# A graph layer's edge scatter: block rows picked from three stacked bfloat16 parts, and the feeding that goes with it

## The chip, the cores and the metric

The kernel runs on one core of a Trainium2 chip. The metric is the device time of one execution in microseconds; a chip run gives it, and a hardware profile of one execution gives the trace.

## The reference

A message-passing layer with 12500 nodes of 64 features, 212500 edges sorted by `dst`, and a hidden width of 128 (float32 throughout):

```python
h = jnp.maximum(_layernorm(x, axis=-1), 0.0)
edge_in = jnp.concatenate([h[src], h[dst], edge_weight1], axis=1)
e = jax.nn.silu(edge_in @ eW1 + eb1)
e = jax.nn.silu(e @ eW2 + eb2)
agg = jax.ops.segment_sum(e, src, num_segments=12500)
out = jax.nn.silu(jnp.concatenate([h, agg], axis=1) @ nW1 + nb1) @ nW2 + nb2
return x + out
```

The edges come sorted by `dst` but the sum runs over `src`, so the kernel has to bring each edge's half-finished row from its place by `dst` to a place by `src`.

## The kernel before

`eW1` is cut in its `src` part, its `dst` part, its weight row and bias. Tables of h times the first two parts are built once per node (`ta` and `tb` in DRAM, and `tb0` for the first nodes; `product` makes them for groups of four tiles of nodes: `first_rows` for `tb0`, `by_edges` and `groups` for the rest).

**Sending.** The edges are taken in 208 blocks of 1024, two to a pair. Since `dst` is sorted, a block's edges need only few rows of `tb`: each quarter of a block (256 edges) has a window of 30 rows. `load_rows` (SP) loads the block's row numbers within the windows, spread over the partitions (`bc`), `windows` loads the window rows (`win`, four transfers a pair), `weights` loads the edge weights as a row of `pick`. `count` (DVE, and PE for `counts`) works out where each edge goes (`to`), and makes `pick`, at L410 for a pair at once: a one-hot matrix of 0 and 1 from `bc`, with the weight row and a row of ones beside it. `send` then works in four pieces per block. PE multiplies `pick` by `win` (`qp`, L477, float32, 64 rows of contraction in two halves): that picks each edge's row of `tb` and adds weight and bias. ACT copies it to the tile `qs` (L486, and a column of places, L487; 16 buffers), and POOL scatters `qs`, 128 edges at a time, to the rows `to` of the array `q` in DRAM (L490, an indirect DMA; 1661 in all).

**Steps.** 450 steps, in 18 levels of 25 batches of nodes, read `q` back by `src` (`qt`, SP), add the rows of `ta`, and run the two layers and the segment sum: `lr` (L598), `oneT` (L603), `pt` (L612, L618), silu (L622), `p` (L650), silu (L654), `seg` (L664), `aggT` (L675).

**What sets the order.** The program order on each engine is written by hand. `turn` lists a step's parts; its empty places (`None`) are where pieces of `send` are put in, so many that the rows which a later level needs are scattered in time. Before the steps begin, 16 blocks are sent, with table building fed in between pieces by counts such as

```python
            for i in range(2, 2 * PIECES):
                next(sending)
                for _ in range(3 if i % PIECES < 3 else 0):
                    next(feed, None)
```

A scatter holds its `qs` buffer and its `to` buffer (four) until it has landed. Each engine works through its own list in order, so an instruction that waits holds up all behind it on that engine.

Of the kernel before, what the change touches and what calls it, by code (L numbers as in the profile page):

```python
# [38 lines left out]
P = 128  # L39
L = 125  # L40
WL = 30
STEP = 15
SPAN = 7 * STEP + WL
# [21 lines left out]
FILL0, FILL_EACH, FILL_LATE = 18, 2, 8  # L65
AFTER = mybir.DependencyInfo(mybir.DependencyClass.Sync, mybir.DependencyReason.DATA)
# [8 lines left out]
def tile_gnn(ctx: ExitStack, tc: tile.TileContext, x, src, dst, ew, eW1, eb1, eW2, eb2, nW1, nb1, nW2, nb2, out):  # L75
# [155 lines left out]
    wins = [const.tile([P, 2, 2, H], F32, name=f"win{i}") for i in range(NW)]  # L231
    nc.vector.memset(wins[0], 0.0)

    def extra_rows(dma, wins):

        for win in wins:
# [69 lines left out]
    qsp = ctx.enter_context(tc.tile_pool(name="qs", bufs=16))  # L306
    top = ctx.enter_context(tc.tile_pool(name="to", bufs=4))
    with ExitStack() as work:
# [19 lines left out]
        def load_rows(s):  # L328

            if s < nblocks:  # L330
# [5 lines left out]
                if g == 0:  # L336
                    bc = ld.tile([P, 2, QR], BF16, name="bc")
                    lists[p] = [bc, None]
                    r = dests[p, 0, 0]
                    of = bass.AP(tensor=r.tensor, offset=r.offset, ap=[[2 * QR, NQR], [0, 32], [1, 2 * QR]])  # L340
                    nc.sync.dma_start(bc.rearrange("p g e -> p (g e)"), of)
                blk[s] = [lists[p][0][:, g]]

        def windows(p):

            table, front, end = (tb, FRONT, NB * P) if 2 * p >= EARLY else (tb0, 0, NE * P)
            if p == 0:
                table, end = tb0[: FRONT + G * P], G * P
            assert 2 * p < EARLY or len(done_b) == NB // G
            at = nc.sync.value_load(base_i[:, p : p + 1], min_val=front, max_val=FRONT + end - SPAN)  # L350
            for a in range(NQR):
# [3 lines left out]
                nc.sync.dma_start(wins[p % NW][a * 32 : a * 32 + WL, :, a % 2, :], of)  # L355

        def load(s):

            if s < nblocks:
                p, g = s // 2, s % 2  # L360
                if g == 0:
                    if p != 1:
                        windows(p)
                    lists[p][1] = ld.tile([P, 2, QR], F32, name="pick")
                blk[s] += [wins[p % NW][:, g], lists[p][1][:, g]]
            if s:
                load_rows(s + 1)

        def weights(s):

            if s < nblocks:
                p, g = s // 2, s % 2
                pick = lists[p][1][:, g]
                e0 = s * BLK
                m = 1 if e0 + 2 * BLK > E else 2
                if m == 2 or e0 + BLK <= E:
                    of = bass.AP(tensor=ew.tensor, offset=ew.offset + e0, ap=[[QR, NQR], [BLK, m], [1, QR]])
                    nc.sync.dma_start(lists[p][1][WL::32, g : g + m, :], of)
                else:
                    for a in range(NQR):  # L380
                        m = min(QR, E - e0 - a * QR)
                        if m > 0:
                            of = bass.AP(tensor=ew.tensor, offset=ew.offset + e0 + a * QR, ap=[[m, 1], [1, m]])
                            nc.sync.dma_start(pick[a * 32 + WL : a * 32 + WL + 1, :m], of)

        def count(s):

            if s < nblocks:
                bc, win, pick = blk[s]
                p, g = s // 2, s % 2  # L390
                whole = p > 0 and (2 * p + 2) * BLK <= E
# [15 lines left out]
                elif not whole:  # L407
                    nc.vector.tensor_scalar(pick, bc, same, plus, op0=OP.is_equal, op1=OP.add)
                elif g == 0:
                    nc.vector.tensor_scalar(lists[p][1], lists[p][0], same, plus, op0=OP.is_equal, op1=OP.add)  # L410
            yield
            if s < nblocks and p and (g == 0 or not whole):
                weights(s)
# [45 lines left out]
        def send(s):  # L459
# [6 lines left out]
            places = locE[:, g * TB : (g + 1) * TB, p].rearrange("p (i a t) -> p i t a", a=2, i=2)  # L466
            for t, i in itertools.product(range(2), range(2)):
                if i or t:
                    yield
                if i == 0:  # L470
# [9 lines left out]
                tiles = [j for j in (4 * i + t, 4 * i + 2 + t) if j < nt]  # L480
# [3 lines left out]
                qp = qps[i]  # L484
# [235 lines left out]
        def first_rows(g):  # L720

            hr = turned(x0, g)
            yield
            got = fp.tile([P, G, H], F32, name="got")
            product(1, hr, mm, "mm", got)
            yield
            nc.scalar.dma_start(tb0[FRONT + g * P : FRONT + (g + G) * P, :].rearrange("(p j) f -> p j f", j=G), got)
# [12 lines left out]
        def products(b0, g, xs):  # L740
# [7 lines left out]
            else:  # L748
                rows_a = fp.tile([P, G, H], F32, name="rows_a")
# [8 lines left out]
            nc.sync.dma_start(tb_buckets[:, b : b + G, :], got)  # L758
# [15 lines left out]
        def destinations():  # L774
# [9 lines left out]
            nc.vector.tensor_scalar(few, part[:NP], 0.5, -float((NE - G) * P), op0=OP.is_lt, op1=OP.mult)  # L784
# [11 lines left out]
            for g in range(2):  # L796
                nc.vector.tensor_tensor(
                    rowsD[:, :, g, :],
# [12 lines left out]
        def first_places():  # L811
# [8 lines left out]
            for at, rows in ((slice(0, 1), G * P), (slice(1, FIRST), NE * P)):  # L820
# [76 lines left out]

        def checks():
# [24 lines left out]
        done_a, done_b, ready, scaled = [], [], set(), set()  # L923
# [321 lines left out]
```

## Time and profile before

| | |
|---|---|
| median of 3 runs | 2332.47 us (2330.95 to 2333.67) |
| the profiled execution | 2332.11 us, span 2330.3 us |
| granted TensorE clock, mean | 0.958 |
| busy | PE 2091.2, PEld 1842.1, DVE 1864.6, ACT 1180.1, POOL 1649.9 us |
| DMA | 401.86 MB, 172 GB/s on the mean |

PE is a matmul's own time and PEld the loading of weights beside it; DVE, ACT and POOL are the vector, scalar and GpSimd engines, SP issues DMAs. A row `A <- B: total, times, longest` of the waits says that an engine's line A stood idle until B ended. "issue" is idle time with nothing to wait for in the trace. A row of the timeline begins with its start and its duration in microseconds.

### The profile page before, as it was taken

What the parts mean: (1) busy time and instruction counts of PE and PEld (TensorE: products, weight loads), DVE (VectorE), ACT (ScalarE), POOL (GpSimd) and SP (SyncE); (2) the same over time, 40 slices, a digit from 0 to 9 for tenths busy, and PEclk for the clock granted to TensorE, in tenths of its full rate; (3) what the DMA queues carried; (4) which work ended last, traced back from release to release, by engine and by line L of the source; (5) the groups of instructions that cost most, each with busy time, mean ns of one, the idle gap of its engine ahead of it and who ended that gap; (6) DMA issues with size and microseconds to landing.
All of it is one profiled execution on the core that took longest, in us unless ns stands there. A gap on an engine that the chain in (4) does not pass through costs nothing.

```text
span 2330.3 us, 49976 instructions
## 1 busy us (share of the span) xinstructions
PE 2091.2 (90%) x17399; PEld 1842.1 (79%) x17399; DVE 1864.6 (80%) x3292; ACT 1180.1 (51%) x3262; POOL 1649.9 (71%) x1711
## 2 busy tenths in 40 slices
PE   3685998889999999998899889999888999999998
PEld 2463677778988888887788778888778888889997
DVE  6975677778888889888888878888888888887664
ACT  3364554445555555554455555555555555555443
POOL 5677777777777777777777777777777777777210
PEclk9766899899999999999999999999999999999999
DMA  4476676555555565555555555555654444444563
GB/s 137 152 240 206 223 248 193 178 185 182 179 179 174 179 180 183 180 174 172 160 169 176 171 169 180 168 169 173 188 168 137 137 138 139 140 139 139 167 211 117
DMA packets 241432, 401.86 MB, mean 172 GB/s; under 512 B 47528, under 2 KB 140195, under 8 KB 240965
## 3 DMA queue, kind: packets, MB, share of 16 engines
q1 hardware_dynamic: 149411, 216.21, 31.6%
q0 software_dynamic: 53568, 123.20, 14.7%
q10 hardware_dynamic: 38192, 59.17, 8.7%
q8 instruction: 139, 2.28, 0.4%
q14 instruction: 122, 1.00, 0.1%
HBM read 191.09 MB, written 207.01 MB: 171 GB/s over the span
## 4 chain that ended last, share of the span: by engine, by line
PE 47%; DMA 20%; DVE 18%; issue 6%; POOL 5%; ACT 3%; SPq 1%; DVEq 0%; ACTq 0%; POOLq 0%
DMA q<-qs,to 14%; PE seg L664 10%; PE pt L618 10%; PE p L650 8%; DMA qt<-q 5%; PE pt L612 5%; PE qp L477 5%; POOL q L490 5%; PE lr L598 3%; DVE one L631 3%; DVE oneT L603 2%; DVE aggT L675 2%; DVE each L400 2%; DVE oh L395 1%; PE ab L215 1%
## 5 line engine op out<-in xcount | busy, mean ns | idle before, releaser
L490 POOL DMA_INDIRECT q<-qs,to x1661 | 1621.8, 976 | 546.2 <-issue 316.8
L622 ACT ACTIVATE e<-pt 128x512 f32<-128x512 f32 x450 | 268.7, 597 | 769.4 <-PE pt L618 680.6
L664 PE MATMUL seg<-one,e 128*128 128x125 f32 x3600 | 496.4, 281 | 34.2 <-DVE aggT L675 24.1
L664 PEld LDWEIGHTS seg<-one,e 128*128 128x128 f32 x3600 | 440.7, 193 | 106.8 <-issue 35.2
L650 PE MATMUL p<-w,e 128*128 128x128 f32 x3600 | 486.7, 278 | 0.0
L650 PEld LDWEIGHTS p<-w,e 128*128 128x128 f32 x3600 | 442.7, 193 | 12.1 <-issue 10.5
L486 ACT COPY qs<-qp 128x256 f32<-128x256 f32 x831 | 308.9, 372 | 221.0 <-PE qp L477 212.6
L675 DVE TENSOR_TENSOR aggT<-aggT,seg 128x500 f32<-128x500 f32 x425 | 284.3, 669 | 87.4 <-PE seg L664 85.7
L603 DVE TENSOR_SCALAR oneT<-lr,part 125x512 f32<-125x512 f32 x450 | 335.2, 745 | 22.9 <-PE lr L598 17.3
L477 PE MATMUL qp<-win,pick 64*128 64x256 f32 x1662 | 318.1, 453 | 14.2 <-ACT qs L486 5.8
L631 DVE TENSOR_TENSOR one<-counts,qt 128x500 f32<-128x500 f32 x450 | 300.9, 669 | 25.6 <-PE counts L434 14.3
L612 PE MATMUL pt<-ident,qt 128*128 128x128 f32 x1800 | 283.7, 281 | 1.5 <-ACT zn L267 1.3
L654 ACT ACTIVATE e<-p 128x512 f32<-128x512 f32 x450 | 269.1, 598 | 30.2 <-PE p L650 18.0
L644 ACT COPY p<-b2f 128x512 f32<-128x512 f32 x450 | 267.7, 595 | 0.0
L618 PE MATMUL pt<-oneT,al 125*128 125x128 f32 x1952 | 264.2, 279 | 0.0
L618 PEld LDWEIGHTS pt<-oneT,al 125*128 125x128 f32 x1952 | 243.6, 196 | 0.0
L449 DVE TENSOR_TENSOR mine<-oh,counts 128x800 f32<-128x800 bf16 x208 | 203.6, 979 | 41.1 <-PE counts L434 41.1
L598 PEld LDWEIGHTS <-qt 128*125 128x125 bf16 x1800 | 156.0, 140 | 84.7 <-DMA qt<-q 49.8
L598 PE MATMUL lr<-identb,qt 128*125 128x128 bf16 x1800 | 185.0, 226 | 39.1 <-DMA qt<-q 37.9
L612 PEld LDWEIGHTS pt<-ident,qt 128*128 128x128 f32 x1800 | 194.8, 144 | 29.3 <-issue 22.5
L451 DVE TENSOR_REDUCE rank<-mine 128x8 f32<-128x800 f32 x208 | 205.1, 986 | 7.2
L400 DVE TENSOR_REDUCE each<-oh 128x100 bf16<-128x800 bf16 x208 | 205.1, 986 | 7.1
(177 smaller groups left out, 1780.4 us busy)
## 6 DMA issues: line engine op xcount, KB each, us to landing
qt<-q SPq DMA_DIRECT2D x450, 288.0 KB
q<-zeros ACTq DMA_DIRECT2D x70, 720.0 KB
q<-qs,to POOLq DMA_INDIRECT x1661
bc<-dests SPq DMA_DIRECT2D x103, 128.0 KB
win<-tb SPq DMA_DIRECT2D x416, 30.0 KB
tb<-got SPq DMA_DIRECT2D x25, 256.0 KB
zd<-zn SPq DMA_DIRECT2D x25, 250.0 KB
zh<-zd SPq DMA_DIRECT2D x25, 250.0 KB
```

The lines of the kernel that those rows point to most:

```text
L477: nc.tensor.matmul(qps[i_][:, :m], pick[half, t * P : (t + 1) * P], win[half, :m], start=True, stop=True)
L486: nc.scalar.copy(qs[:, :m, :H], qp[:, :m, :])
L490: ins = nc.gpsimd.indirect_dma_start(out=q[:], out_offset=bass.IndirectOffsetOnAxis(ap=to[:k, j : j + 1], axis=0), in_=qs[:k, a, :], in_of ...
L598: nc.tensor.matmul(lr[:L, t, :], loc[:, at : at + 1].to_broadcast([P, L]), identb, start=True, stop=True)
L603: nc.vector.tensor_scalar(oneT, st[k].pop("lr")[:L], part1[:L, :], None, op0=OP.is_equal)
L612: nc.tensor.matmul(pt[:, t, :], qt[:, j, :H], ident, is_transpose=True, start=t == 0, stop=False, skip_group_check=True)
L618: nc.tensor.matmul(pt[:, cols, :], a[:L, b, :], oneT[:, cols, :], start=False, stop=True, skip_group_check=True)
L631: nc.vector.tensor_tensor(one.rearrange("p (b j) l -> p b j l", j=n), nodes_p[:, None, None, :].to_broadcast(wide), loc[:, tiles[0][1] : t ...
L650: nc.tensor.matmul(p2[:, t, :], e1[:, t, :], w2, start=False, stop=t == G - 1, skip_group_check=True)
L654: nc.scalar.activation(e2, p2, AF.Silu)
L664: nc.tensor.matmul(item[2][:, b, :], e2[:, t, :], one[:, t, :], start=j < G, stop=j >= G * (n - 1))
L675: nc.vector.tensor_tensor(v, v, seg, op=OP.add)
```

## The change

- `tb` and `tb0` hold, for each row, three bfloat16 numbers that add up to the float32 (`split`: ACT casts, DVE subtracts, ACT casts the rest, DVE subtracts). Block 0 and 1 keep the float32 way from a table of their own (`tbF`, `win0`, `pick0`).
- A pair's windows come in one transfer: 32 rows, each with its three parts, on 96 partitions, eight windows of 128 edges. Its row numbers come on 96 partitions for all 2048 edges (`picks`), and DVE turns them into 0 and 1 in place. Below them, 12 partitions hold three parts of the weights and ones, against three parts of the weight row and the bias (`weighs`, `extra`, made by `first_weights` and `other_weights`).
- A tile of 128 edges then takes one product of 108 rows by 128, in bfloat16.
- `qs` has 9 buffers where it had 16, `rows_a` 2; the lists of `src` and `dst` are cast in place, and `src`'s buffer is loaded again with the weights.
- The feeding counts are others, and `first_weights`, `first_rows` and the rest take turns.

```diff
+    same3 = const.tile([P, 1], F32, name="same3")
+    nc.vector.tensor_scalar(same3, part, -1.0, 1.0 / 3, op0=OP.add, op1=OP.mult)
+    nc.vector.tensor_scalar(same3, same3, float(3 * 2**22), None, op0=OP.add)
+    nc.vector.tensor_scalar(same3, same3, -float(3 * 2**22), None, op0=OP.add)
...
-    tb = dram.tile([P * NB, H], F32, name="tb")
-    dests = dram.tile([NP, NQR, 2, QR], BF16, name="dests")
-
-    tb0 = dram.tile([FRONT + P * NE, H], F32, name="tb0")
+    tb = dram.tile([P * NB, 3 * H], BF16, name="tb")
+    dests = dram.tile([NP, 2 * NQR, QR], BF16, name="dests")
+    weighs = dram.tile([4, NP * PAIR], BF16, name="weighs")
+    extra = dram.tile([12, H], BF16, name="extra")
...
+    def split(*pairs_):
+
+        with nc.allow_low_precision("three parts hold every bit"):
+            for parts, v in pairs_:
+                nc.scalar.copy(parts[0], v)
+            yield
+            for parts, v in pairs_:
+                nc.vector.tensor_tensor(v, v, parts[0], op=OP.subtract)
+            yield
+            for parts, v in pairs_:
+                nc.scalar.copy(parts[1], v)
+            yield
+            for parts, v in pairs_:
+                nc.vector.tensor_tensor(parts[2], v, parts[1], op=OP.subtract)
...
+    wins = [const.tile([P, 2 * NQR, H], BF16, name=f"win{i}") for i in range(NW)]
+    picks = [const.tile([P, PAIR], BF16, name=f"pick{i}") for i in range(NW)]
...
-    qsp = ctx.enter_context(tc.tile_pool(name="qs", bufs=16))
+    qsp = ctx.enter_context(tc.tile_pool(name="qs", bufs=9))
...
-                    bc = ld.tile([P, 2, QR], BF16, name="bc")
-                    lists[p] = [bc, None]
-                    r = dests[p, 0, 0]
-                    of = bass.AP(tensor=r.tensor, offset=r.offset, ap=[[2 * QR, NQR], [0, 32], [1, 2 * QR]])
-                    nc.sync.dma_start(bc.rearrange("p g e -> p (g e)"), of)
-                blk[s] = [lists[p][0][:, g]]
+                    r = dests[p, 0]
+                    of = bass.AP(tensor=r.tensor, offset=r.offset, ap=[[0, 3 * WT], [1, PAIR]])
+                    nc.sync.dma_start(picks[p % NW][: 3 * WT], of)
+                    if p > 1:
+                        weights(p)
+                blk[s] = [None]
+
+        def weights(p):
+
+            assert p in weighed
+            w = weighs[0, p * PAIR : (p + 1) * PAIR]
+            of = bass.AP(tensor=w.tensor, offset=w.offset, ap=[[NP * PAIR, 4], [0, 3], [1, PAIR]])
+            nc.sync.dma_start(picks[p % NW][3 * WT : K3], of)
...
+            if p:
+                rows = table[bass.ds(at - front, SPAN), :]
+                of = [[H, 3 * WT], [STEP * 3 * H, 2 * NQR], [1, H]]
+                of = bass.AP(tensor=rows.tensor, offset=rows.offset, ap=of)
+                nc.sync.dma_start(wins[p % NW][: 3 * WT], of)
+                return
...
-                    nc.vector.tensor_scalar(lists[p][1], lists[p][0], same, plus, op0=OP.is_equal, op1=OP.add)
-            yield
-            if s < nblocks and p and (g == 0 or not whole):
-                weights(s)
+                    both = picks[p % NW][: 3 * WT]
+                    nc.vector.tensor_scalar(both, both, same3[: 3 * WT], None, op0=OP.is_equal)
...
+                if p:
+                    i, t = t, i
+                    qp = mm.tile([P, 2, H], F32, name="qp", tag="mm")
+                    for a, j in enumerate(range(4 * i + 2 * t, min(4 * i + 2 * t + 2, nt))):
+                        nc.tensor.matmul(
+                            qp[:, a], pick[:K3, j * P : (j + 1) * P], win[:K3, 2 * i + t], start=True, stop=True
+                        )
...
+            got3 = fp.tile([P, G, 3, H], BF16, name="got3", bufs=2)
+            yield from split(([got3[:, :, c] for c in range(3)], got))
+            nc.sync.dma_start(to, got3.rearrange("l j c h -> l (j c h)"))
...
-                rows_a = fp.tile([P, G, H], F32, name="rows_a")
+                rows_a = fp.tile([P, G, H], F32, name="rows_a", bufs=2)
...
-            nc.sync.dma_start(tb_buckets[:, b : b + G, :], got)
+            got3 = fp.tile([P, G, 3, H], BF16, name="got3", bufs=2)
+            yield from split(([got3[:, :, c] for c in range(3)], got))
+            nc.sync.dma_start(tb_buckets[:, b : b + G, :], got3.rearrange("l j c h -> l j (c h)"))
...
+        def first_weights():
+
+            w4 = lp.tile([P, 4, P], BF16, name="w4")
+            nc.vector.memset(w4[:, 3].bitcast(F32), TWO_ONES)
+            xt3 = lp.tile([2, 3, H], BF16, name="xt3")
+            yield from split(([w4[:, c] for c in range(3)], wF), ([xt3[:, c] for c in range(3)], xt))
+            to = bass.AP(tensor=weighs.tensor, offset=weighs.offset, ap=[[P, P], [NP * PAIR, 4], [1, P]])
+            nc.sync.dma_start(to, w4)
+            weighed.update(range(FIRST))
+            of = xt3.rearrange("k c h -> k (c h)")
+            of0 = bass.AP(tensor=of.tensor, offset=of.offset, ap=[of[0:1].ap[0], [0, 3], [1, 3 * H]])
+            nc.sync.dma_start(extra[:9].rearrange("(i j) h -> i (j h)", i=3), of0)
+            nc.sync.dma_start(extra[9:].rearrange("(i j) h -> i (j h)", i=1), of[1:2])
+            yield
+            for win in wins:
+                of = bass.AP(tensor=extra.tensor, offset=extra.offset, ap=[[H, 12], [0, 2 * NQR], [1, H]])
+                nc.sync.dma_start(win[3 * WT : K3], of)
+            yield
+
+        def other_weights():
+
+            lists_in(sf, ew, nc.sync.dma_start)
+            wR = sf
+            m = PAIR // 8
+            w4s = [lp.tile([NP, 4, m], BF16, name=f"w4{i}") for i in range(2)]
+            yield
+            for w4 in w4s:
+                nc.vector.memset(w4[:, 3].bitcast(F32), TWO_ONES)
+            for c in range(8):
+                v, w4 = wR[:, c * m : (c + 1) * m], w4s[c % 2]
+                yield from split(([w4[:, c_] for c_ in range(3)], v))
+                to = weighs[0, FIRST * PAIR + c * m :]
+                to = bass.AP(tensor=to.tensor, offset=to.offset, ap=[[PAIR, NP - FIRST], [NP * PAIR, 4], [1, m]])
+                nc.sync.dma_start(to, w4[FIRST:])
+                yield
+            weighed.update(range(FIRST, NP))
...
-            f, sf = (lp.tile([NP, PAIR], F32, name=n) for n in ("f", "sf"))
+            f, sf = dstR.bitcast(F32), srcR.bitcast(F32)
...
-            feed = itertools.chain(far, *(first_rows(g) for g in range(G, NE, G)))
+            others = [first_rows(g) for g in range(G, NE, G)]
+            feed = turns([table, first_weights(), itertools.chain(far, others[0])] + others[1:], 3)
...
+            nc.sync.dma_start(wF, bass.AP(tensor=ew.tensor, offset=ew.offset, ap=[[P, P], [1, P]]))
+            nc.sync.dma_start(xt[0:1], eW1[2 * D : 2 * D + 1, :])
+            nc.sync.dma_start(xt[1:2], rows_of(eb1, 1))
+            nc.sync.dma_start(tb0[:FRONT], zeros.bitcast(BF16)[:FRONT, : 3 * H])
...
-                for _ in range(3 if i % PIECES < 3 else 0):
+                for _ in range(6):
                     next(feed, None)
+                if i == 5:
+                    windows(1)
+                    weights(1)
...
-                for _ in range(4 if i % PIECES < 3 else 0):
+                for _ in range(5 if i % PIECES < 3 else 1):
...
-            for _ in range(3 if (done - 1) % PIECES < 3 else 0):
+            for _ in range(4 if (done - 1) % PIECES < 3 else 0):
```

At the start on ACT, from block 0's second piece (`qs<-qp`, then `qs<-locE`) on. Before:

```order
L486 COPY qs<-qp 128x2x128
L487 COPY qs<-locE 128x2x16
L808 CAST base_i<-lot 1x96
L486 COPY qs<-qp 128x2x128
L487 COPY qs<-locE 128x2x16
L698 ACTIVATE x_199<-cen 128x768
L703 ACTIVATE var<-var 128x12
L486 COPY qs<-qp 128x2x128
L487 COPY qs<-locE 128x2x16
```

and now, from the third piece on (`got_403` is the first split's, `w_406` the weights', `xt_408` the weight row's and bias's):

```order
L518 COPY qs<-qp 128x2x128
L519 COPY qs<-locE 128x2x16
L222 CAST got_403<-got 128x4x128
L222 CAST w_406<-wF 128x128
L222 CAST xt_408<-xt 2x128
L228 CAST got_403<-got 128x4x128
L730 ACTIVATE x_208<-cen 128x768
L518 COPY qs<-qp 128x2x128
L519 COPY qs<-locE 128x2x16
L228 CAST w_406<-wF 128x128
L228 CAST xt_408<-xt 2x128
```

Between the third and the fourth piece of block 0 now stand four casts besides the activation on `x`.

On SP, from the write of the row numbers on (`rowsD` to `dests`). Before:

```order
L804 DMA dests<-rowsD 104x2048
L341 DMA bc<-dests 128x1x512
L240 DMA win_144<-in_L_gnn_eW_dram 2x2x128 x2
L240 DMA win_144<-in_L_gnn_eb_dram 2x2x128 x2
L240 DMA win_145<-in_L_gnn_eW_dram 2x2x128 x2
L240 DMA win_145<-in_L_gnn_eb_dram 2x2x128 x2
L341 DMA bc<-dests 128x1x512
L378 DMA pick<-in_edge_weight_dram 4x2x256
```

and now:

```order
L844 DMA dests<-rowsD 104x2048
L365 DMA pick_154<-dests 96x2048
L1097 DMA wF<-in_edge_weight_dram 128x128
L1098 DMA xt<-in_L_gnn_eW_dram 1x128
L1099 DMA xt<-in_L_gnn_eb_dram 1x128
L1100 DMA tb_140<-zeros 16x384
L765 DMA tb_140<-got_403 128x1536
L945 DMA weighs<-w_406 128x4x128
```

The loads of `wF` (the first weights), `xt` and the clearing of `tb` stand behind the load of the row numbers, which waits for `dests`; then the split rows and weights are written.

On PE, in the middle of the steps, a piece of `send` with what stands beside it. Before, one for two pieces:

```order
L612 MATMUL pt<-ident,qt 128x128 x4
L618 MATMUL pt<-oneT,al_4568 128x128 x4
L477 MATMUL qp<-win_143,pick 128x256 x2
L650 MATMUL p_18003<-w_96,e_17998 128x128 x4
L664 MATMUL seg<-one,e_18009 128x125 x4
```

and now, each piece its own:

```order
L650 MATMUL pt<-oneT,al_5492 128x128 x4
L682 MATMUL p_12938<-w_96,e_12920 128x128 x4
L497 LDWEIGHTS pick_153
L497 MATMUL qp<-win_150,pick_153 128x128
L497 LDWEIGHTS pick_153
L497 MATMUL qp<-win_150,pick_153 128x128
L437 LDWEIGHTS rest
L437 MATMUL counts<-each,rest 128x100
L696 MATMUL seg<-one,e_12944 128x125 x4
```

The two float32 products of 256 columns have become, piece by piece, two loads of 128 columns of `pick` with a product of 128 columns each, and stand at each of the four pieces instead of at every second.

More of the change, by code (lines that the diff above doesn't have):

```diff
@@ L230, in tile_gnn, with extra_rows @@
     NW = 3
[L231 to L236, printed above, removed]
+    wins = [const.tile([P, 2 * NQR, H], BF16, name=f"win{i}") for i in range(NW)]
+    picks = [const.tile([P, PAIR], BF16, name=f"pick{i}") for i in range(NW)]
+    def extra_rows(dma, win):
+        if True:
             for i, row in enumerate((eW1[2 * D : 2 * D + 1, :], eb1)):
@@ L347, in windows @@
             if p == 0:
+                table, end = tbF, G * P
+            if p == 1:
                 table, end = tb0[: FRONT + G * P], G * P
@@ L363, in load @@
                         windows(p)
-                    lists[p][1] = ld.tile([P, 2, QR], F32, name="pick")
-                blk[s] += [wins[p % NW][:, g], lists[p][1][:, g]]
+                if p:
+                    blk[s] += [wins[p % NW][:, g * NQR : (g + 1) * NQR], picks[p % NW][:, g * BLK : (g + 1) * BLK]]
+                else:
+                    blk[s] += [win0[:, g], pick0[:, g]]
             if s:
                 load_rows(s + 1)
[L369 to L384, printed above, removed]
         def count(s):
@@ L483, in send @@
                     continue
-                qp = qps[i]
+                if not p:
+                    qp = qps[i]
                 qs = qsp.tile([P, 2, W], F32, name="qs")
@@ L992, in tile_gnn @@
             next(firsts)
-            list(table)
+            next(table)
+            next(table)
             list(firsts)
@@ L1167, in tile_of @@
                 )
-                nc.vector.tensor_tensor(pre[:n], pre[:n], got[:n], op=OP.add)
+                for c in range(1 + 2 * k):
+                    nc.vector.tensor_tensor(pre[:n], pre[:n], got[:n, c * H : (c + 1) * H], op=OP.add)
             sf = gw.tile([P, 1], F32, name="gsf")
```

54 lines of the change are left out of this document (32 added, 22 removed).

## The prediction

> **What bounds the kernel now.** I read the page first (busy time by engine, the costliest groups), then what POOL waited for, then POOL's scatter line over stretches of the span. On the page, groups read: engine, operation, count, then busy microseconds and mean nanoseconds of one, then idle time before them.
>
> ```profile
> PE 2091.2 (90%) x17399; PEld 1842.1 (79%) x17399; DVE 1864.6 (80%) x3292; ACT 1180.1 (51%) x3262; POOL 1649.9 (71%) x1711
> L490 POOL DMA_INDIRECT q<-qs,to x1661 | 1621.8, 976 | 546.2 <-issue 316.8
> ```
>
> PE looks like the bound (90%) and POOL idle by a third. But POOL's idle time is in slivers. Its waits (total, times, longest) and the scatter's minimum/median/maximum:
>
> ```profile
> POOL q L490 <- issue: 316.8, 1039, 0.3
> POOL q L490 <- DMA q<-qs,to: 76.5, 251, 0.3
> POOL q L490 <- ACT qs L487: 60.9, 114, 4.7
> L490 POOL DMA_INDIRECT q<-qs,to x1661: 887/958/1676, 21.2 to 2177.5; - x185
> ```
>
> 316.8/1039 = 0.305 us stands before each scatter though nothing is late: a fixed gap. So one scatter costs 0.96 + 0.305 = 1.265 us, and 1661 of them cost 2101 us; they run from 21.2 to 2177.5, which is 2156. Over stretches (PE, PEld, DVE, ACT, POOL, then clock, DMA share, GB/s):
>
> ```profile
> 400.00:600.00 200.00, 180.53 (x1486) 159.75 (x1485) 160.76 (x279) 98.88 (x277) 152.06 (x158) 0.95 0.59 182
> 600.00:800.00 200.00, 196.70 (x1742) 178.01 (x1741) 176.33 (x305) 111.24 (x301) 152.43 (x157) 1.00 0.58 178
> 1000.00:1200.00 200.00, 181.36 (x1551) 160.39 (x1550) 164.25 (x288) 101.58 (x284) 152.74 (x156) 0.99 0.56 171
> 2082.00:2331.00 249.00, 236.69 (x2091) 227.69 (x2089) 158.42 (x286) 114.41 (x236) 83.20 (x93) 0.99 0.52 158
> ```
>
> POOL does 156 to 158 scatters per 200 us whether PE has 180 or 197 us of work: 157 × 1.265 = 199 us, so POOL is full, and it sets the pace until about 2100. Only from about 2082 does PE (237 of 249 us) set the end. What holds work back in the middle is behind POOL:
>
> ```profile
> DVE to L453 <- DMA q<-qs,to: 163.8, 85, 6.1
> L490 POOL DMA_INDIRECT q<-qs,to x1594: 954/958/1676, 21.2 to 2081.8; - x200
> L486 ACT COPY qs<-qp x807: 353/372/419, 20.3 to 2080.6; 128x256 f32<-128x256 f32 x162
> ```
>
> The last two count the tile `qs` up to 2082 us: ACT has filled 807 × 2 = 1614 rows of scatter when POOL has issued 1594, a lead of 20.
>
> **The change, part by part.** *The products.* One half block of float32 products, then the bfloat16 `lr` group, which has the new products' shape within three partitions:
>
> ```profile
> 1211.47 0.70 PE L477 MATMUL qp<-win,pick 64*128 64x256 f32 x4
> 1212.10 1.16 PE L664 MATMUL seg<-one,e 128*128 128x125 f32 x8
> 1213.10 0.39 PE L598 MATMUL lr<-identb,qt 128*125 128x128 bf16 x4
> 1213.33 0.28 PE L612 MATMUL pt<-ident,qt 128*128 128x128 f32 x1
> ```
>
> 1211.47 to 1212.10 is 0.63 us per half block, 1.26 per block. Four bfloat16 products take 0.23 (start to start) to 0.39 us (busy), so eight take 0.46 to 0.78; I take 0.62. PE loses 0.64 × 208 = 133 us of work, but beside POOL: nothing comes off the time before 2082. Scatters keep their number and size.
>
> *The end.* After 2082 POOL has 67 scatters left; 20 of them were already produced, so 47 (5.9 blocks) fall in PE's own stretch: 5.9 × 0.64 = −3.8 us. Against it, nine `qs` tiles hold 18 rows; with some three in flight the lead is at most 15 instead of 20, so PE enters its last stretch 5 × 1.265 = 6.3 us later against POOL. Net +2 (−4 to +6).
>
> *The new pick operation on DVE.* Here is the first price. A DVE operation can hold a scatter up:
>
> ```profile
> 62.81 0.54 DVE L410 TENSOR_SCALAR pick<-bc,same,plus 128x512 f32<-128x512 bf16 x1
> 63.01 1.17 POOL L490 DMA_INDIRECT q<-qs,to  x1 [0.30 <-issue]
> 28.05 0.96 DVE L694 TENSOR_TENSOR cen<-x,mean 128x768 f32<-128x768 f32 x1
> 28.16 1.68 POOL L490 DMA_INDIRECT q<-qs,to  x1 [0.30 <-issue]
> ```
>
> L410 ends at 63.35, and the scatter that began inside it takes 0.21 us more than its usual 0.96; L694, with two inputs in SBUF, adds 0.72. The scatter seems to need something soon after its start and to wait until the operation ends. For an operation of length d at a random phase of a 1.265 us period that costs about d²/2.53. Groups of DVE operations (count, busy, mean ns):
>
> ```profile
> L410 DVE TENSOR_SCALAR pick<-bc,same,plus 128x512 f32<-128x512 bf16 x102 | 56.7, 556 | 0.0
> L408 DVE TENSOR_SCALAR pick<-bc,same,plus 128x256 f32<-128x256 bf16 x2 | 0.8, 412 | 0.0
> L395 DVE TENSOR_TENSOR oh<-numbers,bkB 128x800 bf16<-128x800 bf16 x208 | 118.0, 567 | 0.0
> L694 DVE TENSOR_TENSOR cen<-xs,mean 128x768 f32<-128x768 f32 x8 | 7.7, 966 | 0.3
> ```
>
> L410 would give 102 × 0.122 = 12.5 and L395 208 × 0.127 = 26.4: 39 us. The trace has (976 − 958) ns × 1661 = 30 us over the median, so I scale by 0.77. The new operation, 96x2048 in place from bfloat16 to bfloat16, is not in this trace. Upper bound: the slope from L408 to L410, 144 ns for 256 elements, gives 0.556 + 1536 × 0.00056 = 1.42 us. Lower: bfloat16 all through halves the time of an element from L694 to L395 (1.26 to 0.71 ns), and half the slope gives 0.14 + 2048 × 0.00028 = 0.71. I take 0.71, since both its sides are bfloat16 as in L395. Cost: 102 × 0.77 × (0.71² − 0.556²)/2.53 = +6 us; at 1.42 us +53; if it holds nothing, −10.
>
> The Trainium skill, "VectorE: DVE Perf Modes", section on the perf-mode tier table, has 0.693 us for a bfloat16 `tensor_scalar` of 2048 elements in SBUF; by that the term stays +6. The Trainium skill, "SBUF — State Buffer", section "Who interferes with whom", says that such an operation holds the port pair it shares with GpSimd to its end and fully blocks the other: a rule against this change. The trace agrees at 63.01 (1.17 us), except that the page infers that `tensor_tensor` leaves descriptor writing alone, and L694 did not (1.68 us); by the page alone the next term would be 0 and the sum 6 us less.
>
> *The splits.* 29 groups of rows, two subtractions of 128x512 each, both inputs in SBUF. From L694, 0.966 × 512/768 = 0.64 us plus a start: 0.69. 58 × 0.77 × 0.69²/2.53 = +8; eight of them fall in the start, where POOL isn't full, and sixteen more of 104x256 add 1: I take +6, between 0 (POOL is hit by nothing) and +11. The casts are ACT's, with 51% busy: nothing.
>
> *Loads.* Per pair SP sends three transfers where six went before, but 628 KB for 264 (windows 196 for 120, destinations 384 for 128, weights 48 for 16): 38 MB more over the run, about a tenth, on a DMA share of 0.56 to 0.59. With every wait of a scatter for a DMA at most 0.3 us I put this at 0, up to +10.
>
> *The start.* Here is the largest term.
>
> ```profile
> 23.98 0.32 SPq L804 DMA_DIRECT2D dests<-rowsD  x1
> 30.37 0.60 SPq L341 DMA_DIRECT2D bc<-dests  x1
> 31.23 0.35 ACT L486 COPY qs<-qp 128x256 f32<-128x256 f32 x1
> 31.97 1.43 POOL L490 DMA_INDIRECT q<-qs,to  x1 [2.14 <-ACT qs L487]
> 36.91 0.96 POOL L490 DMA_INDIRECT q<-qs,to  x1 [2.25 <-ACT qs L487]
> 56.14 0.96 POOL L490 DMA_INDIRECT q<-qs,to  x1 [4.70 <-ACT qs L487]
> 70.29 0.95 POOL L490 DMA_INDIRECT q<-qs,to  x1 [3.57 <-ACT qs L487]
> ```
>
> SP waits 6.4 us for `dests` to land before the next issue, so `wF`, now behind `pick<-dests`, is issued at about 31.0 and lands (0.6 to 6.4 us later; I take 2.5) at 33.5. ACT's order puts the casts of `got`, `wF` and `xt`, the next cast of `got` and a centred square ahead of block 0's last copy: that starts at about 36.5, not 31.2, and its scatter at 38, not 32. Block 1 then needs both splits finished, `weighs` and `extra` written and read back, `tb0` written and read, and the pick operation: two such trips of 2.5 to 5 us behind the casts put its first scatter near 49 instead of 36.9. Blocks 2 and 3 wait for more splits on ACT and DVE and for `srcR`, loaded a second time behind the lists (62 for 56.1, 80 for 70.3). From there on POOL is full, so it keeps the delay: +11 us, +4 if the second blocks catch up in the stalls they had anyway (4.7 and 3.6 us here), +20 if each trip takes 6.4.
>
> **The sum.** Against the profiled execution's own 2332.1 us (2332.47 is the median of the runs, so one scale serves): 2332 + 11 + 6 + 6 + 2 = 2357 us. Adding the small ends (+4, −10, 0, −4) gives 2322, the large ones without the pick's bound (+20, +6, +11, +10, +6) 2385. A measurement of this kernel can tell about 0.2%, 4.7 us, from no change.
>
> **The rivals.** *The pick operation at the long bound* (12%): if it costs 1.42 us, longer than a scatter's period, each of the 102 holds one up, by 0.61 us on the mean where it is 0.15 in the sum: 2357 + 47 = 2404. For it: 2048 elements, in place. Against it: L395's rate.
>
> *Nine `qs` tiles starve someone* (12%): before, DVE took the back pressure (163.8 us at L453). With nine tiles ACT takes it, at the copy, and the activations behind it on ACT hold PE's steps. It decides once PE's steps between two blocks take longer than the remaining lead of 15 × 1.265 = 19 us. If a third of the 163.8 us comes back as idle time on POOL: +55, 2412. Against it: PE has 133 us less to do.
>
> *PE was the bound where both are full* (8%): from 600 to 1000 PE is busy 98%. If its order, not POOL, set that pace, its 39 blocks × 0.64 come off, 25 us: 2307 if the start costs nothing. It needs POOL's gaps there to be waits; they are the same 0.305 us as where PE is at 90%.
>
> *Nothing to be measured* (10%): the start's delay is caught up and the pick holds nothing, 2328 to 2337. That the change isn't what it says is no case: its order has one 128x128 product per tile.
>
> The forecast, 2357 (2338 to 2380), has 58%. The range leaves out the faster case (8%), half of the even case (5%) and half of the starving case (6%): 2332 to 2406. Faster 8%, same 10%, slower 82%.
>
> **What would show it.** Right: POOL still does about 156 scatters per 200 us with gaps of 0.305 us; the mean of a scatter rises from 976 to about 983 ns; PE's busy time falls by about 130 us with its share in the middle under 92%; the seventh scatter starts near 38 us and block 1's first near 49; the pick operation takes about 0.7 us. Wrong: a scatter count per 200 us above 160, POOL waits of over 1 us in the middle for ACT's `qs`, a pick operation of 1.4 us, or a first hundred microseconds as before.

## The result, and the profile after

The changed kernel takes 2368.37 us (median of 4 runs, 2364.36 to 2371.53) where the kernel before takes 2333.07; the ratio is 1.0154 (95% interval 1.0140 to 1.0168). The forecast was 2357 (2338 to 2380 with 58%, 2332 to 2406 in all), slower with 82%. The profiled execution took 2371.53 us, its span is 2369.7: 39.4 us more than the span of before, somewhat more than the medians' 35.3. In two sets of runs below, the first and the second, the kernel before took 2986 and 2979 us for a reason that stays open (the record names for the first set the same chip as for a later set in which it took 2332.41), so a time is held only against the kernel before of its own set.

From the page of the changed kernel, busy time by engine and the groups of the scatter, the copy and the new products:

```profile
PE 1950.1 (82%) x17398; PEld 1840.5 (78%) x17398; DVE 1932.8 (82%) x3373; ACT 1214.2 (51%) x3340; POOL 1679.0 (71%) x1711
L522 POOL DMA_INDIRECT q<-qs,to x1661 | 1651.2, 994 | 556.7 <-issue 329.2
L518 ACT COPY qs<-qp 128x256 f32<-128x256 f32 x831 | 310.5, 374 | 772.0 <-DMA q<-qs,to 624.2
L497 PE MATMUL qp<-win,pick 108*128 108x128 bf16 x1645 | 237.1, 230 | 77.7 <-ACT qs L518 67.4
```

PE lost 141 us of work (2091.2 to 1950.1) and the time rose. POOL's scatters are as many, 18 ns longer each (29.4 us in all), with 10.5 us more idle time between them. ACT, not DVE, now waits for landed scatters (624.2 us). POOL's waits and the scatter's own row:

```profile
POOL q L522 <- issue: 329.2, 1080, 0.3
POOL q L522 <- ACT qs L519: 67.2, 130, 14.3
POOL q L522 <- DMA q<-qs,to: 50.0, 164, 0.3
L522 POOL DMA_INDIRECT q<-qs,to x1661: 887/959/2727, 24.5 to 2217.2; - x185
```

The fixed gap is still 329.2/1080 = 0.305 us. The first scatter is 3.3 us later than before, the last 39.7. The middle and the stretch after the last scatter (PE, PEld, DVE, ACT, POOL, clock, DMA share, GB/s), first of the changed kernel:

```profile
600.00:800.00 200.00, 180.84 (x1750) 176.26 (x1749) 180.37 (x303) 112.19 (x301) 152.58 (x156) 1.00 0.66 199
1000.00:1200.00 200.00, 165.97 (x1519) 157.04 (x1518) 164.75 (x284) 100.22 (x283) 152.55 (x156) 0.97 0.61 185
2217.20:2369.70 152.50, 142.77 (x1239) 139.49 (x1237) 87.03 (x166) 64.08 (x113) 19.06 (x26) 0.98 0.56 172
```

and the same stretch of the kernel before:

```profile
2177.50:2330.30 152.80, 141.54 (x1228) 138.27 (x1226) 86.36 (x165) 63.43 (x113) 19.10 (x26) 0.98 0.57 173
```

From 600 to 800 PE has fallen from 196.70 to 180.84 of 200 us, and POOL does 156 scatters where it did 157. After the last scatter both kernels need the same 152.5 to 152.8 us. So all of the loss lies before the last scatter, on POOL.

I followed the start of each scatter through both traces (counted over all 1661 records). At scatter 150 the changed kernel is 23.5 us late: 13.9 of it gaps, 9.6 longer scatters. From there to scatter 1640 the gaps add nothing (13.85) and the longer scatters go on to 29.4. At the end 3.6 us of gaps come back.

### The profile page after: what moved, and what is told of

It is laid out like the page before. It is cut to its first block, busy times and chain, and to the rows that moved or that the text cites. A ratio compares the mean times of both kernels' runs of the same rounds, so it can differ in the third digit from the quotient of the medians.

```text
span 2369.7 us, 49260 instructions
## 1 busy us (share of the span) xinstructions
PE 1950.1 (82%) x17398; PEld 1840.5 (78%) x17398; DVE 1932.8 (82%) x3373; ACT 1214.2 (51%) x3340; POOL 1679.0 (71%) x1711
## 2 busy tenths in 40 slices
DMA packets 294667, 448.41 MB, mean 189 GB/s; under 512 B 124438, under 2 KB 181569, under 8 KB 294104
## 4 chain that ended last, share of the span: by engine, by line
DMA 31%; PE 24%; DVE 18%; POOL 11%; issue 10%; ACT 6%; ACTq 0%; SPq 0%; POOLq 0%; DVEq 0%
DMA q<-qs,to 26%; POOL q L522 11%; PE pt L650 5%; PE seg L696 5%; PE p L682 5%; DMA qt<-q 4%; PE pt L644 3%; ACT qs L518 2%; DVE oneT L635 2%; DVE rank L473 2%; DVE mine L471 2%; DVE one L663 2%; DVE aggT L707 2%; PE lr L630 1%; DVE each L425 1%
## 5 line engine op out<-in xcount | busy, mean ns | idle before, releaser
L522 POOL DMA_INDIRECT q<-qs,to x1661 | 1651.2, 994 | 556.7 <-issue 329.2
L518 ACT COPY qs<-qp 128x256 f32<-128x256 f32 x831 | 310.5, 374 | 772.0 <-DMA q<-qs,to 624.2
L682 PE MATMUL p<-w,e 128*128 128x128 f32 x3600 | 501.8, 283 | 18.5 <-ACT p L676 18.3
L682 PEld LDWEIGHTS p<-w,e 128*128 128x128 f32 x3600 | 453.0, 197 | 26.7 <-ACT p L676 22.7
L696 PEld LDWEIGHTS seg<-one,e 128*128 128x128 f32 x3600 | 447.0, 195 | 27.7 <-issue 17.3
L644 PE MATMUL pt<-ident,qt 128*128 128x128 f32 x1800 | 289.2, 285 | 50.7 <-ACT qs L518 43.2
L497 PE MATMUL qp<-win,pick 108*128 108x128 bf16 x1645 | 237.1, 230 | 77.7 <-ACT qs L518 67.4
L497 PEld LDWEIGHTS <-pick 108*128 108x128 bf16 x1645 | 160.0, 104 | 116.6 <-issue 108.8
```

Of the source, the lines that this page charges most:

```text
L497: nc.tensor.matmul(qp[:, a], pick[:K3, j * P : (j + 1) * P], win[:K3, 2 * i + t], start=True, stop=True)
L518: nc.scalar.copy(qs[:, :m, :H], qp[:, :m, :])
L522: ins = nc.gpsimd.indirect_dma_start(out=q[:], out_offset=bass.IndirectOffsetOnAxis(ap=to[:k, j : j + 1], axis=0), in_=qs[:k, a, :], in_of ...
L644: nc.tensor.matmul(pt[:, t, :], qt[:, j, :H], ident, is_transpose=True, start=t == 0, stop=False, skip_group_check=True)
L682: nc.tensor.matmul(p2[:, t, :], e1[:, t, :], w2, start=False, stop=t == G - 1, skip_group_check=True)
L696: nc.tensor.matmul(item[2][:, b, :], e2[:, t, :], one[:, t, :], start=j < G, stop=j >= G * (n - 1))
```

## The experiments

**Is PE's time worth anything?** The kernel before, with its products made from the upper halves of the same float32 numbers (the lower halves are left out, so the picked rows are rounded):

```diff
-                                qps[i_][:, :m], pick[half, t * P : (t + 1) * P], win[half, :m], start=True, stop=True
+                                qps[i_][:, :m],
+                                pick.bitcast(BF16)[half, 2 * t * P + 1 : 2 * (t + 1) * P : 2],
+                                win[half, :m].bitcast(BF16)[:, :, 1::2],
+                                start=True,
+                                stop=True,
```

> The kernel before, with the products qp made from the upper halves of the same float32 tiles (truncated to bfloat16, same shapes, loads and order, so the picked rows are rounded): PE loses about three quarters of its 318 us there (more than the 133 us that the change saves) and nothing else changes. Theory (POOL paces until 2100 us): only PE's last stretch gains, at most 5.9 blocks x 0.95 us = 6 us, so 2326 to 2333 where the kernel before takes 2333. Rival (PE was the bound where both were full): 25 us and more come off, below 2308.

2323.72 us beside 2330.45 (ratio 0.9965, 0.9951 to 0.9979). Its busy times, and two stretches:

```profile
PE 1950.4 (84%) x16568; PEld 1776.7 (77%) x16568; DVE 1860.8 (80%) x3292; ACT 1162.1 (50%) x3262; POOL 1646.9 (71%) x1711
```

```profile
600.00:800.00 200.00, 186.09 (x1694) 174.26 (x1694) 179.51 (x312) 110.54 (x303) 152.19 (x157) 1.00 0.60 180
1000.00:1200.00 200.00, 167.64 (x1471) 154.96 (x1470) 164.42 (x288) 100.43 (x287) 152.24 (x157) 0.97 0.56 170
```

PE's busy time is that of the changed kernel (1950.4 and 1950.1), and 141 us less work on PE brought 6.7 us. POOL does 157 scatters per 200 us all the same. PE was no bound in the middle, not even where it was 98% busy.

**Are nine `qs` buffers the cost?** One number in the kernel before:

```diff
-    qsp = ctx.enter_context(tc.tile_pool(name="qs", bufs=16))
+    qsp = ctx.enter_context(tc.tile_pool(name="qs", bufs=9))
```

> The kernel before with 9 qs buffers where it had 16, now beside a kernel before that POOL paces (2332). First theory (a shorter lead costs only in PE's last stretch): 0 to +8 us, POOL's gaps at 0.305 us, ACT's copy waiting for landed scatters instead of DVE's L453. Rival (nine buffers starve POOL or hold up ACT and so PE): +20 us or more, with POOL gaps of over 1 us in the middle.

2337.69 us beside 2332.01 (1.0026, 1.0015 to 1.0037): 5.7 us. What POOL and ACT waited for:

```profile
POOL q L490 <- issue: 321.1, 1053, 0.3
POOL q L490 <- ACT qs L487: 65.8, 115, 4.7
```

```profile
ACT qs L486 <- DMA q<-qs,to: 404.8, 246, 6.2
```

The wait moves from DVE (163.8 us) to ACT (404.8 us) and POOL's gaps stay as they were. Scatter by scatter, the two kernels are within 3.1 us of each other up to number 1640, where the run with nine buffers is 1.9 us ahead, and its last one is 3.0 us late: 4.8 us of gaps come in at the last 21 scatters. So the cost arises in PE's last stretch, as forecast (6.3).

**What lengthens the scatters, and what makes the start late?** Four edits of the changed kernel. The pick operation with an accumulated sum (`picked`, a small new tile, is not used):

```diff
-    nc.vector.tensor_scalar(both, both, same3[: 3 * WT], None, op0=OP.is_equal)
+    nc.vector.tensor_scalar(both, both, same3[: 3 * WT], 0.0, op0=OP.is_equal, op1=OP.add, accum_out=picked[: 3 * WT])
```

the pick operation in quarters:

```diff
-    nc.vector.tensor_scalar(both, both, same3[: 3 * WT], None, op0=OP.is_equal)
+    for h_ in range(4):
+        part4 = both[:, h_ * (PAIR // 4) : (h_ + 1) * (PAIR // 4)]
+        nc.vector.tensor_scalar(part4, part4, same3[: 3 * WT], None, op0=OP.is_equal)
```

and the start: the loads of `wF`, `xt` and `tb0`'s front stand ahead of `load_rows(0)` (first test); also `extra_rows(nc.sync.dma_start, win0)` stands behind the list of `dst` (second test). The kernel before with nine buffers ran beside them in both sets.

> The kernel before with 9 qs buffers where it had 16, and nothing else. Theory (POOL paces; a shorter lead costs only in PE's last stretch): 0 to +8 us on 2333, at most the 5 x 1.265 us by which PE enters its last stretch later; POOL's gaps stay at 0.305 us, and the waits for landed scatters move from DVE's L453 to ACT's qs copy. Rival (nine buffers starve POOL or hold up ACT and so PE): +20 us or more, with POOL gaps of over 1 us in the middle.

> The changed kernel, with the pick operation (same operands, 96x2048 bfloat16 in place) in the form that also writes an accumulated sum, which should be slower: from 0.71 ns (L395) to 1.26 ns (L694) an element, 1.5 to 2.6 us instead of 0.74. Theory a (only an operation that takes both port pairs holds POOL's scatter): the pick's 26 us of scatter excess vanish, about 2342. Theory b (any DVE operation with SBUF operands holds a scatter for as long as it lasts): every pick meets a scatter, excess 60 to 130 us, 2400 to 2470. Rival (the scatters are longer because of the greater DMA traffic, not because of DVE): unchanged, 2368.

> The changed kernel, with the pick operation cut in four of 512 columns each, estimated at 0.25 to 0.3 us apiece. Theory (DVE holds the scatter until the operation ends, so the cost goes with the square of its length): the pick's 26 us fall to 8 to 14, total 2350 to 2358, mean scatter 984 to 988 ns. Rival (DMA traffic lengthens the scatters): unchanged, 2368, mean 994 ns.

> The changed kernel, with the loads of wF, xt and the clearing of tb0's front issued on SP ahead of the first windows, not behind the load of the row numbers. Theory (ACT's 11.15 us wait for wF holds block 0's last copy and pushes all later scatters): the seventh scatter starts near 33 us instead of 43, and as POOL keeps any delay, the end comes 5 to 10 us earlier, 2358 to 2363. Rival (block 1's weights and rows, written and read back, are late anyway): the seventh scatter is early but the thirtieth isn't, 2366 to 2369.

In this set and the second one POOL isn't full, so that their times answer no question on a kernel that POOL paces. Two rows of the kernel before with nine buffers in the first set show it: POOL waits 518.0 us for ACT's copies (65.8 in the run above), and ACT stands idle for 348.6 us in waits that no event of the trace ends (`remote`):

```profile
POOL q L490 <- ACT qs L487: 518.0, 204, 6.6
```

```profile
ACT e L622 <- remote: 348.6, 60, 9.2
```

The second set:

> The kernel before with 9 qs buffers where it had 16, beside a kernel before at about 2331 us. Theory (POOL paces; a shorter lead costs only in PE's last stretch): 0 to +8 us. Rival (nine buffers starve POOL or hold up ACT and so PE): +20 us or more, with POOL gaps of over 1 us in the middle.

> The changed kernel with the pick operation in the form that also writes an accumulated sum. On the slower chip it took longer than the plain form there and DVE had 161 us more to do. Theory a (only an operation that takes both port pairs holds a scatter): the pick's 26 us of scatter excess vanish, about 2342, mean scatter 978 ns. Theory b (any long DVE operation on SBUF holds it): each pick meets a scatter, 2400 to 2470, mean scatter over 1020 ns. Rival (the greater DMA traffic lengthens the scatters): unchanged, 2368, mean 994 ns.

> The changed kernel with the pick operation cut in four of 512 columns. Theory (DVE holds the scatter until the operation ends, so the cost goes with the square of its length): the pick's 26 us fall to 8 to 14, total 2350 to 2358, mean scatter 984 to 988 ns. Rival (DMA traffic lengthens the scatters): unchanged, 2368, mean 994 ns.

> The changed kernel with two moves on SP: the loads of wF, xt and the clearing of tb0's front ahead of the first windows, and the list of dst loaded ahead of the extra rows of win0, whose buffer is cleared late. Theory (POOL keeps whatever the start loses): the first scatter is back near 21 us, the seventh near 32, the thirtieth 10 to 13 us earlier than in the changed kernel, and the end too: 2355 to 2360. Rival (the blocks after the first wait for the splits written and read back in any case): the seventh early, the thirtieth less than 4 us earlier, 2364 to 2368.

| against the kernel before, same set | ratio (95% interval) |
|---|---|
| 9 buffers, first and second set | 0.9994 (0.9974 to 1.0015), 1.0011 (0.9989 to 1.0032) |
| pick with sum | 0.9879 (0.9825 to 0.9933), 0.9895 (0.9841 to 0.9950) |
| pick in quarters | 0.9858 (0.9822 to 0.9893), 0.9833 (0.9791 to 0.9875) |
| start order, first test, second test | 0.9745 (0.9718 to 0.9772), 0.9759 (0.9715 to 0.9804) |

The expected times rest on a POOL that is full and can't be held against these. Three things can be read. First, where POOL is not full, all these versions of the change are faster than the kernel before, by about 1 to 2.6%. The changed kernel itself ran in neither set, so what each edit is worth there can't be told, nor how much of it is PE's 141 us. Second, the seventh scatter starts at 33.2 us in the first start test and at 31.9 in the second, where the changed kernel has 43.0 and the kernel before 32.0; the thirtieth starts at 79.9 and 78.2 (78.6 in the run with both repairs below), where they have 89.2 and 74.2. So the start's rival, that the later blocks are late in any case, falls, though 4 to 6 us of the delay stay. Third, what holds a single scatter can still be seen, instruction by instruction. Here are the changed kernel's pick operation, the comparison `oh` ahead of it, and the scatters beside them; then the form with the sum (second set):

```profile
1001.24 0.56 DVE L420 TENSOR_TENSOR oh<-numbers,bkB 128x800 bf16<-128x800 bf16 x1
1001.46 1.17 POOL L522 DMA_INDIRECT q<-qs,to  x1 [0.30 <-issue]
1001.84 0.99 DVE L425 TENSOR_REDUCE each<-oh 128x100 bf16<-128x800 bf16 x1
1002.74 0.74 DVE L434 TENSOR_SCALAR pick<-pick,same 96x2048 bf16<-96x2048 bf16 x1
1002.94 1.37 POOL L522 DMA_INDIRECT q<-qs,to  x1 [0.30 <-DVE each L425]
```

```profile
1017.93 2.33 DVE L435 TENSOR_SCALAR_CACHE_REDUCE pick<-pick,same 96x2048 bf16<-96x2048 bf16 x1
1018.68 0.96 POOL L523 DMA_INDIRECT q<-qs,to  x1 [0.30 <-issue]
1019.95 0.96 POOL L523 DMA_INDIRECT q<-qs,to  x1 [0.30 <-issue]
```

The plain form, 0.74 us, makes its scatter 0.41 us longer. The form with the sum lasts three times as long (2.33 us), and a scatter that runs wholly inside it takes its 0.96. The count bears it out: in each of the two sets, the form with the sum goes with 2 of 103 picks that lengthen a scatter (by more than 0.04 us), 0.15 us in all, and the plain form of the start tests with 79 and 78, 20.9 and 15.6 us in all. Theory a holds for the instruction, theory b falls: it is the form, not the length alone, that holds POOL. That is the rule of the Trainium skill, "SBUF — State Buffer", section "Who interferes with whom", which leaves out the form that writes its accumulator; here the trace agrees (0.96 us).

**Both repairs, beside a kernel before that POOL paces.** The second start test and the quarters in one kernel:

> The changed kernel with both repairs: the start order on SP (wF, xt, tb0's front and the list of dst earlier) and the pick operation in four of 512 columns. If the first theory holds (start +14 us and pick +16 us are kept by POOL, which sets the pace), both come off: scatter 30 is 10 to 12 us earlier than in the changed kernel, the pick's excess is 2 to 6 us where it was 26, the mean scatter 980 to 984 ns, total 2332 to 2342, within 0.4% of the kernel before. Rival (what costs is the DMA traffic or the nine qs buffers, which are as in the changed kernel): not below 2355.

2336.91 us beside 2332.41 (1.0022, 1.0012 to 1.0031). Its scatter and its pick operation, its seventh scatter, and the changed kernel's pick operation:

```profile
L524 POOL DMA_INDIRECT q<-qs,to x1661 | 1621.9, 976 | 548.9 <-issue 317.4
L436 DVE TENSOR_SCALAR pick<-pick,same 96x512 bf16<-96x512 bf16 x412 | 127.9, 370 | 0.0
31.93 0.95 POOL L524 DMA_INDIRECT q<-qs,to  x1 [0.64 <-ACT w L228]
```

```profile
L434 DVE TENSOR_SCALAR pick<-pick,same 96x2048 bf16<-96x2048 bf16 x103 | 78.0, 757 | 0.0
```

The mean scatter is back at 976 ns, though DVE has 50 us more to do in the pick (127.9 for 78.0) and the DMA traffic and the nine buffers are those of the changed kernel. The rival of this run falls: 2336.9, not over 2355. As differences of the medians to each run's own kernel before, 4.5 us are left of 35.3: the two repairs take back 30.8. Between the two profiled spans, 2369.7 and 2333.1 us, shorter scatters make up 29.3 us; of the start's 13.9 us of gaps at scatter 150, 6.1 are left. The equal mean is a balance: up to scatter 150 the scatters are still 9.9 us longer than in the kernel before, and from there on 9.8 us shorter.

**Can it be beaten?** The same kernel, with `oh` and each subtraction of `split` in two halves:

> The changed kernel with both repairs and with shorter DVE operations elsewhere: the comparison oh (128x800, two inputs in SBUF) and each subtraction of the splits cut in two. If a scatter is held in proportion to the square of the holding operation's length, oh's 13.4 us of excess fall to 4 to 7 and the splits' 5.6 to 2 to 3; POOL keeps every microsecond, so 2337 falls by 8 to 12, to 2325 to 2330, under the kernel before (2332). If the short operations hold as much in all, or DVE becomes the bound by its added 30 us, 2336 to 2345.

2334.00 us beside 2330.74 (1.0012, 1.0003 to 1.0021). Beside its own kernel before that is 3.3 us, where the run with both repairs has 4.5: 1.2 us gained, not 8 to 12, and not clear of noise, as the two intervals overlap. Neither of the two ranges was met. The scatter's group, a row of POOL's timeline, and DVE's row for the operation `cen`:

```profile
L536 POOL DMA_INDIRECT q<-qs,to x1661 | 1613.5, 971 | 556.1 <-issue 326.0
155.33 1.19 POOL L536 DMA_INDIRECT q<-qs,to  x1 [3.08 <-ACT qs L533]
152.32 0.96 DVE L740 TENSOR_TENSOR cen<-xs,mean 128x768 f32<-128x768 f32 x1
```

and that row in the run with both repairs:

```profile
149.08 0.96 DVE L728 TENSOR_TENSOR cen<-xs,mean 128x768 f32<-128x768 f32 x1
```

The scatters did give 8.4 us (1621.9 to 1613.5). But up to scatter 150 the gaps are 5.8 us more than in the run with both repairs, and most of the gain goes there. POOL waits 1.59 us at 149.82 and 3.08 us at 155.33 for ACT's copies, where the other run has its fixed 0.3 at the same scatters. ACT's copies stand in its list behind work that waits for DVE, and DVE is 3.2 us late: `cen` starts at 152.32, not 149.08, after 128.7 us of work, not 124.9. POOL in turn comes to the first of these scatters 1.6 us earlier. The halves themselves make that work: two halves of a split's subtraction of 128x512 take 0.75 us where the whole takes 0.68. So shorter operations cost time on DVE, and at the start, where POOL has no stock, that is paid. Whether halving `oh` alone would have kept the gain wasn't tried. No version of the change that was tried beats the kernel before where POOL paces.

## Why the prediction was right, term by term

The mechanism was right: POOL paces the run, PE's relief is hidden behind it, and what delays a scatter is kept almost to the end (13.9 us of gaps at scatter 150 are 13.9 still at 1640). That the time fell into the range is in part luck: the largest miss, 14.4 us on the pick operation, was met by 5.9 us the other way at the end. The terms against the two profiled executions, in microseconds; "other longer scatters" and "end" are what is left when the counted terms are taken off:

| term | forecast | measured |
|---|---|---|
| start | +11 | +13.9 |
| pick operation | +6 | +20.4 |
| splits | +6 | +5.7 |
| other longer scatters | 0 | +3.3 |
| end | +2 | −3.9 |
| sum | +25 | +39.4 (medians +35.3) |

**The start** was right in its course and small by 3 us. Rows of the changed kernel on SP, ACT and POOL:

```profile
24.71 0.32 SPq L844 DMA_DIRECT2D dests<-rowsD  x1
35.13 0.31 SPq L365 DMA_DIRECT2D pick<-dests  x1
35.49 0.42 SPq L1097 DMA_DIRECT2D wF<-in_edge_weight_dram  x1
38.61 0.30 ACT L222 CAST w<-wF 128x128 bf16<-128x128 f32 x1 [11.15 <-DMA wF<-in_edge_weight_dram]
43.02 0.96 POOL L522 DMA_INDIRECT q<-qs,to  x1 [11.08 <-ACT w L228]
52.49 0.97 POOL L522 DMA_INDIRECT q<-qs,to  x1 [7.25 <-ACT hr L749]
```

From the issue of the write of `dests` to the load behind it SP took 10.4 us where it took 6.4 before, which wasn't foreseen and stays open, so `wF` was issued at 35.5, not 31.0; ACT stood 11.15 us at its cast; the seventh scatter came at 43.0 (forecast 38), block 1's first at 52.5 (49). I had not seen that the extra rows of `win0` wait for a buffer that is now cleared late, and delay the list of `dst` behind them (issued at 8.4 us, not 6.4). With these loads moved, in the run with both repairs, the seventh scatter starts at 31.93; block 1's first, at 41.4, is still 4.5 us behind the kernel before.

**The pick operation** is the term that was mis-sized, and by the hold, not by the operation: 0.757 us on the mean where 0.71 was forecast. I had charged it by a random phase, d²/2.53, scaled by 0.77 to fit the rows of before. Counted over the records, 101 of 103 picks lengthen a scatter by more than 0.04 us (63 of 102 before), by 30.8 us in all (10.4 before).

The hold itself is simple. A scatter that begins under the pick is held for the rest of the operation less 0.13 us, in both kernels: before, 0.34 us were left and 0.21 held; now 0.54 are left and 0.41 held. What failed is the random phase. In the rows at 1001.24 us above, `oh` holds a scatter, `each` and the pick follow `oh` without a pause, and the next scatter begins 0.2 us after the pick. This repeats: in the kernel before 40 of the 102 picks, and now 41 of the 103, meet a scatter about 0.2 us after their start, and in 31 of these, in each kernel, the scatter ahead was longer too, while a random phase would put two into that window of 0.02 us. That the hold by `oh` sets the phase is read from these rows and wasn't tried apart. No scatter begins earlier under a pick, so each of these costs the pick's length less 0.33 us, and that doubled: 8.4 us in all before, 17.4 now. The others that begin under the pick went from 1.3 to 8.4 us; 1.8 of it is one scatter at 117.49 us that the split's subtractions behind the pick hold too.

A scatter also seems to need the resource twice, since picks that start 0.27 to 0.45 us after a scatter's start lengthen it as well, by 0.17 to 0.36; that second moment had cost the old, shorter operation at most 0.09 (0.7 us in all before, 5.0 now). So a price fitted on the sum over short operations was carried to a longer one, where the records of before, scatter by scatter, would have given the 0.41. In quarters of 0.37 us, hardly longer than that 0.33, the scatters that begin under the pick are longer by 4.4 us in all, 3.4 of it in two scatters that a split's subtraction behind the pick holds too; the whole operation had 25.8.

**The splits** (scatters that begin under one of their subtractions) and the edits that were put at nothing came as forecast. PE lost 141 us (133 forecast) and is 90% busy where it was 98%; casts and the tenth of DMA traffic more (448.41 for 401.86 MB) cost nothing that shows: the median scatter is 959 ns where it was 958. The 46.6 MB more were forecast as 38.

**The end** had the wrong sign by a little: nine buffers do cost 5.7 us, but PE's relief brings 6.7, more than the 3.8 forecast. Together that is −1.0; the other 2.9 us are not traced to anything, and the medians of the kernel before differ by as much as 2.6 us between the sets in which POOL paces.

**The rivals.** The long pick operation (1.42 us) falls by its row, 0.74; that each pick would hold a scatter, which the rival needed that length for, came true all the same (101 of 103, 0.30 us on the mean where the sum had 0.15). Nine buffers starving someone falls by the run that changed them alone. PE as the bound falls by the run that relieved PE alone. That nothing could be measured falls by the result.

## What to carry to other kernels

An engine at 71% can set the pace when its idle time is a fixed gap before each of its instructions: count the instructions per stretch, and see whether that number moves with the load of the others. Work taken off another engine then pays only where the pacing engine has run out, and each sliver added to its instruction, or to its first one, is paid almost in full. Price an operation that holds it by the single records, not by an average over phases: here 41 of 103 picks met a scatter at the same moment. Beside a POOL that issues indirect DMAs, four short DVE operations cost less than one long one here, even though they take longer in sum, as long as DVE has that time to give; at the start of this kernel it hasn't. The form with the sum holds nothing, but what it is worth where POOL paces wasn't measured.

## What the runs showed of the hardware that I had not expected

- How long a DVE operation lasts says little on what it costs POOL: 2.33 us in one form hold nothing, 0.74 us in another hold 0.41.
- The hold is the rest of the operation less 0.13 us, and the operation doesn't meet the scatters at random: some 40 of 100 picks meet one 0.2 us after their start, in both kernels. So 0.2 us more of length (0.54 to 0.74) doubled the hold of those from 0.21 to 0.41 us.
